# A graph layer's sorted edge groups, taken in ten pairs and in quarters instead of one by one and in halves

## The chip, the cores and the metric

The kernel runs on one core of a Trainium2 chip. The time is the device time of one execution in microseconds, as the median of several runs. The engines are TensorE (PE in the profile, its weight loads PEld), VectorE (DVE), ScalarE (ACT), GpSimd (POOL) and SyncE (SP). Each has a queue of its own and works through it in order.

## The reference

There are 6,250 nodes with 128 features and 100,000 edges, sorted by their destination `dst`. Each edge has a source `src` and four attributes.

```python
msg_in = concatenate([x[src], x[dst], edge_attr], axis=1)
h = silu(msg_in @ mW1 + mb1)
messages = h @ mW2 + mb2
aggregated = segment_sum(messages, dst, num_segments=N)
u = silu(concatenate([x, aggregated], axis=1) @ uW1 + ub1)
updated = u @ uW2 + ub2
out = layernorm(x + layer_norm(x + updated, ln_g, ln_b))
```

## The kernel before

**Tables.** The product with mW1 is split by rows of mW1: the source part of all nodes is a table `A` (and `tab_a` in memory), the destination part with the bias a table `tab_b`. An edge's hidden row is the silu of its row of `A`, its row of `tab_b` and the product of its attributes.

**Groups.** The edges are cut into 98 groups of 1,024 (`G` = 8 tiles of 128). 78 of them are *listed* groups: GpSimd gathers their rows of `tab_a` by eight indirect DMAs a group (`fetch`, line 244), the destination and attribute parts are products of a window of 80 rows of `tab_b` with a matrix of zeros and ones (`before_rows`, tile `pre`), VectorE adds both (`hidden`, line 665) and ScalarE takes the silu (line 667). Every other of GpSimd's gathers is tied to one of TensorE's products (`paced`), so that gathers go on with the products.

**Sorted groups.** The other 20 groups, every fourth from 15 to 91, have no gather. Their edges were sorted by source on the chip, in order over four rows of 256, and their rows of `A` are selected by products. `A` is held in three bf16 parts (`parts_of`). The windows of sorted positions in which the 128 nodes of block `b` can fall are given by `window`; for each the three parts are multiplied by a mask `O` of zeros and ones, and the sums collect in the bank `po`. `picks` makes the masks: two rows of four by VectorE (line 1065), two by ScalarE with a Square and one common Relu (lines 1069 and 1070). `sorted_matrices` (lines 1047 and 1056) compares for the destinations (`st`) and for the edges' places (`Oc`); `attribute_part` brings the attributes into sorted order by a product with `Oc` and masks it into `st` (line 1081); `begin_half` opens `po` with the destination and attribute parts; `select` runs the selection; `sorted_hidden` takes the silu of `po` (line 1112); `turned_hidden` transposes it back to rows of edges (`h_s`, line 1121); `sorted_oh` makes the matrix for the sums by destination.

**Sums.** `sums` multiplies a group's hidden rows by its matrix `oh` into the tile `pt` (80 columns, or 104 for listed groups; beside them the transposed degrees, when they are due), and `add` adds it into the nodes' sums (`acc`, line 713) and counts (line 707).

**Order.** The order is written out by hand (`manual_schedule`): one stage of the loop (line 1225) for each listed group `g`. In a stage the engines' queues get, in this order: loads and gathers for groups some stages ahead; `matrices` of the listed group two ahead; `before_rows` and `hidden` of the next one; the sorted groups' steps (`sorted_before`); the sums of `g`; more of the sorted groups' steps (`sorted_behind`); and the steps of a batch of 512 nodes (`node_stage`: `node_u`, `node_y` and `node_z` in three following stages, and for a later batch `load_x`, `turned_x` and `make_b`). With one sorted group to three listed ones, each sorted group's steps are spread over six stages; `d` is how many stages are left until its sums. At `d` = 3 the first half is selected (48 and 36 products), at 2 the third quarter of the masks (39), at 1 the fourth (45). At `d` = 0 its sums stand ahead of those of `g`.

**Banks.** The product tiles are `pre` (three banks), `pn` (two, function `bank`), `po` and `pt` (one each).

Names of products in the profile: line 152 is the helper `matmul`, line 155 the helper `transpose`.

Of the kernel before, what the change touches and what calls it, by code (L numbers as in the profile page):

```python
# [10 lines left out]
F32 = mybir.dt.float32  # L11
# [16 lines left out]
def kernel(  # L28
# [57 lines left out]
    Q0, QD, QN = 15, 4, 20  # L86
    by_sort = {Q0 + QD * q: q for q in range(QN)}
# [6 lines left out]
    SORTED = Q0 - 7  # L94
    S0 = 96
    HB = GE // 2
    SLACK = 400.0
# [13 lines left out]
    def made_for(g):  # L111
        stage = stage_of(g) - 5 if g in by_sort else turn_of(g) - LEAD
        return max(k for k in range(NB) if k < 2 or x_stage(k) + 2 < stage)
# [5 lines left out]
    def window(b, half):  # L119
# [4 lines left out]
        lo = max(floor(edge(b * P, -1)), half * HB)  # L124
        hi = min(ceil(edge(min(b * P + P - 1, N - 1), 1)) + 1, half * HB + HB)
        return lo, hi
# [48 lines left out]

    def narrow():
        return ps1.tile([P, 2 * P], F32, name="pt")
# [396 lines left out]
    for k in range(NST + 1):  # L574
        ohbuf.append(kept.tile([P, G, WS if k < NST else W], F32, name=f"oh{k}"))
# [258 lines left out]
    def turned_lists():  # L834
        pt = selected()
        for f, of in enumerate((src_i, rel)):
            picked = first.tile([P, QN, G], F32, name="picked")
            nc.vector.tensor_copy(picked, of[:, Q0 : Q0 + QN * QD : QD, :])
# [135 lines left out]
    def prepare():  # L974
        pool = edges.enter_context(tc.tile_pool(name="sel", bufs=1, side="right"))
        t = {
            "O": lambda: pool.tile([P, G // 2, HB], BF16, name="O", bufs=3),
            "sc": lambda: pool.tile([P, 2, GE], F16, name="sc", bufs=2),
            "ar": lambda: pool.tile([P, GE], F16, name="ar"),
            "h": lambda: pool.tile([P, G, H], F32, name="h_s"),  # L980
            "hT": lambda: pool.tile([P, HB], F32, name="hT", bufs=2),
        }
        t["Oc"] = pool.tile([P, GE], F32, name="Oc")
        t["st"] = pool.tile([P, GE], F32, name="st_s")
        t["mv"] = [pool.tile([P, H], F32, name=f"mv_s{k}") for k in range(2)]
        t["at"] = pool.tile([P, P], F32, name="at_s")
        nc.vector.memset(t["st"][S0 - 32 : S0], 0.0)
        for m in t["mv"]:
            nc.vector.memset(m[S0 - 32 : S0], 0.0)
        nc.vector.memset(t["at"][:, :S0], 0.0)  # L990
# [34 lines left out]
    def load_sorted(g):  # L1025
        t, q = sel[0], by_sort[g]
        cols = slice(q * GE, (q + 1) * GE)
        now["sc", g] = t["sc"]()
        nc.sync.dma_start(
            now["sc", g], sd[0:2, cols].rearrange("(o f) e -> o f e", o=1).to_broadcast([P, 2, GE])  # L1030
        )
        now["ar"] = t["ar"]()
        nc.sync.dma_start(now["ar"][:W], sd[3:4, cols].to_broadcast([W, GE]))
        nc.sync.dma_start(now["ar"][S0:], sd[2:3, cols].to_broadcast([P - S0, GE]))
        nc.sync.dma_start(
            t["at"][:, S0:],
            edge_attr[g * GE : (g + 1) * GE].rearrange("(c a) d -> c (a d)", a=G),
        )

    def load_rows(g):  # L1040
        t, q = sel[0], by_sort[g]
        need_bases(g)
        nc.sync.dma_start(t["mv"][q % 2][:W], tab_b[bass.ds(bases[g], W), :])

    def sorted_matrices(g):
        t = sel[0]
        nc.vector.tensor_scalar(
            t["st"][:W],
            now["ar"][:W],
            p_col[:W],  # L1050
            0.0,
            op0=OP.is_equal,
            op1=OP.add,
            accum_out=deg_col(g),
        )
        nc.vector.tensor_scalar(t["Oc"], now["sc", g][:, 1], p_col, None, op0=OP.is_equal)

    def picks(g, c):
        half, r0 = c // 2, c % 2 * (G // 2)
        O = sel[0]["O"]()  # L1060
        key = now["sc", g][:, 0, half * HB : (half + 1) * HB]
        for j in range(G // 2):
            r = r0 + j
            if j < 2:
                nc.vector.tensor_scalar(  # L1065
                    O[:, j], key, p_rows[:, r : r + 1], None, op0=OP.is_equal
                )
            else:
                nc.scalar.activation(O[:, j], key, AF.Square, bias=p_less[:, r : r + 1])  # L1069
        nc.scalar.activation(O[:, 2:], O[:, 2:], AF.Relu, bias=ones[:, 0:1], scale=-1.0)  # L1070
        now[c] = O
# [4 lines left out]
    def attribute_part(half):  # L1076
        t = sel[0]
        cols = slice(half * HB, (half + 1) * HB)
        px = bank().rearrange("p i f -> p (i f)")
        matmul(px, t["at"], t["Oc"][:, cols], start=True, stop=True)  # L1080
        nc.vector.scalar_tensor_tensor(
            t["st"][S0:, cols], now["ar"][S0:, cols], part[S0:], px[S0:],
            op0=OP.is_equal, op1=OP.mult,
        )

    def begin_half(g, half):
        t = sel[0]
        now["po"] = selected()
        matmul(
            now["po"], t["mv"][by_sort[g] % 2], t["st"][:, half * HB : (half + 1) * HB], start=True, stop=False  # L1090
        )

    def select(c):
        half, r0 = c // 2, c % 2 * (G // 2)
        O, po = now.pop(c), now["po"]
        todo = []
        for b in range(NT):
            if r0 <= b % G < r0 + G // 2:
                lo, hi = window(b, half)
                if lo < hi:  # L1100
                    todo.append((b, lo - half * HB, hi - half * HB))
        for i, (b, lo, hi) in enumerate(todo):
            for a in parts_of(b):
                last_one = c % 2 == 1 and i == len(todo) - 1 and a.tensor is sel[0]["low"].tensor
                matmul(
                    po[:, lo:hi], a, O[:, b % G - r0, lo:hi],
                    start=False, stop=last_one, share=1 / 3,
                )

    def sorted_hidden(half):  # L1110
        now["hT", half] = sel[0]["hT"]()
        nc.scalar.activation(now["hT", half], now.pop("po"), AF.Silu)  # L1112

    def turned_hidden(g, half):
        if half == 0:
            h_s[g] = sel[0]["h"]()
        px = bank().rearrange("p i f -> p (i f)")
        hT = now.pop(("hT", half))
        for i in range(G // 2):
            transpose(px[:, i * P : (i + 1) * P], hT[:, i * P : (i + 1) * P], ident)  # L1120
        nc.scalar.copy(
            h_s[g][:, half * G // 2 : (half + 1) * G // 2].rearrange("p i f -> p (i f)"), px
        )

    def sorted_oh(g):
        oh[g] = ohbuf[NST]
        nc.vector.tensor_tensor(
            oh[g][:, :, :W],
            w_row[:, None, :].to_broadcast([P, G, W]),
            rel_s[:, by_sort[g], :, None].to_broadcast([P, G, W]),  # L1130
            op=OP.is_equal,
        )

    def sorted_ahead(j):
        for k in by_sort:
            if j == stage_of(k) - 6:
                load_sorted(k)
            if j == stage_of(k) - 5:
                load_rows(k)

    def sorted_first(j):
        for k in by_sort:
            if stage_of(k) == j:
                turned_hidden(k, 1)

    def sorted_before(j):
        for k in by_sort:
            d = stage_of(k) - j
            if d in (5, 4, 3, 2):
                picks(k, 5 - d)  # L1150
        for k in by_sort:
            if stage_of(k) == j:
                add(k, sums(k))
        for k in by_sort:
            d = stage_of(k) - j
            if d == 4:
                attribute_part(0)
            if d == 3:
                begin_half(k, 0)
                select(0)  # L1160
                select(1)
                sorted_hidden(0)
            if d == 2:
                turned_hidden(k, 0)
                begin_half(k, 1)
                select(2)
            if d == 1:
                select(3)
                sorted_hidden(1)
                sorted_oh(k)  # L1170

    def sorted_behind(j):
        for k in by_sort:
            d = stage_of(k) - j
            if d == 4:
                attribute_part(1)
        for k in by_sort:
            d = stage_of(k) - j
            if d == 5:
                sorted_matrices(k)  # L1180
# [44 lines left out]
    for j, g in enumerate(listed):  # L1225
# [19 lines left out]
        sorted_first(j)  # L1245
# [320 lines left out]
```

## Time and profile before

| | us |
|---|---|
| median of 3 runs (lowest, highest) | 1009.2 (1008.7, 1020.3) |
| profiled execution, its time | 1011.3 |
| its span, first to last instruction | 1009.2 |
| TensorE busy in the span | 802.7 |
| GpSimd busy in the span | 611.0 |
| VectorE busy in the span | 583.9 |
| ScalarE busy in the span | 459.0 |

The mean granted clock of TensorE is 0.893 over the span. Rows of groups of instructions give the line, engine, operation, output<-input, shapes and count, then busy us and the mean ns of one, then the engine's idle time just before them and what ended it. Rows of waits give who waited for whom, us in total, times, and the longest one. Rows of a window give its start and end, its length, each engine's busy us with the number of instructions, TensorE's granted clock, the busy share of the DMA engines and GB/s. Rows of the timeline give start, length, engine, line and what was done how many times in a row; those of the chain give start, length and what stood in the chain. "issue" is time in which an engine waited for nothing that the profile shows.

### The profile page before, as it was taken

The page shows a single profiled execution, that of the slowest core. Times are in us where ns is not written, and L with a number is a line of the kernel's source. Part 1 is how long each engine was busy: PE and PEld are TensorE (multiplying, and loading weights), DVE is VectorE, ACT ScalarE, POOL GpSimd, SP SyncE. Part 2 cuts the span into 40 slices and gives each one's busy share as a digit, 9 for nine tenths or more (in the row PEclk, how much of TensorE's full clock was granted, in tenths as well). Part 3 has the DMA queues.
Part 4 walks back from the last instruction along what each step waited for, and adds up shares of the span by engine and source line. Part 5 has one row for each costly group of instructions (what it writes and reads, how often), then busy time and mean ns, then how long its engine had stood idle before and what let it go on. Part 6 is the DMA issues. An engine that isn't in the chain of part 4 may idle for free.

```text
span 1009.2 us, 19469 instructions
## 1 busy us (share of the span) xinstructions
PE 802.7 (80%) x7141; PEld 694.4 (69%) x7141; DVE 583.9 (58%) x1467; ACT 459.0 (45%) x690; POOL 611.0 (61%) x633
## 2 busy tenths in 40 slices
PE   4557546778988978978889878988888889888784
PEld 4547546667867777767768777777777677677673
DVE  3465687964654654745655664763754664664473
ACT  1122113563545545545554554563554554453343
POOL 6656655866666666665666566666665666675550
PEclk8769777889999989989999999989999989998875
DMA  9543222442333433432332432432432423321220
GB/s 228 156 107 99 77 59 80 112 114 64 112 93 87 115 89 90 113 88 79 110 111 66 126 104 64 127 102 72 130 90 76 124 81 96 96 78 51 67 57 26
DMA packets 87784, 96.27 MB, mean 95 GB/s; under 512 B 22070, under 2 KB 63622, under 8 KB 87682
## 3 DMA queue, kind: packets, MB, share of 16 engines
q1 hardware_dynamic: 54410, 47.59, 16.2%
q0 software_dynamic: 19904, 40.80, 16.1%
q10 hardware_dynamic: 13368, 6.56, 2.4%
q8 instruction: 58, 0.95, 0.4%
q14 instruction: 44, 0.36, 0.1%
HBM read 83.26 MB, written 11.63 MB: 94 GB/s over the span
## 4 chain that ended last, share of the span: by engine, by line
PE 63%; issue 14%; DVE 13%; ACT 4%; another core or an unknown queue 3%; DMA 1%; DVEq 1%; POOL 0%; ACTq 0%; SPq 0%; POOLq 0%
PE po L152 22%; PE pt L152 16%; PE pre L152 12%; PE pn L152 9%; PE pn L155 2%; DVE ga L665 1%; ACT O L1069 1%; ACT O L1070 1%; DVE y L773 1%; DVE bn L726 1%; DVE z L798 1%; DVE deg L707 1%; DVE st L613 1%; ACT h L667 1%
## 5 line engine op out<-in xcount | busy, mean ns | idle before, releaser
L244 POOL DMA_INDIRECT ga<-tab_a,src_i x582 | 570.7, 981 | 348.1 <-issue 163.4
L152 PE MATMUL po<-O,A_low 128*128 128x144 bf16 (+25 forms) x1120 | 208.7, 226 | 20.3 <-issue 20.0
L152 PE MATMUL po<-O,A 128*128 128x147 bf16 (+37 forms) x1720 | 174.3, 227 | 39.0 <-issue 20.3
L152 PE MATMUL pre<-mv,st 128*128 128x128 f32 x1244 | 178.0, 292 | 28.6 <-issue 7.8
L152 PEld LDWEIGHTS pre<-mv,st 128*128 128x128 f32 x1244 | 163.8, 206 | 41.0 <-issue 21.1
L152 PEld LDWEIGHTS pt<-oh,h 128*128 128x128 f32 x1244 | 170.2, 215 | 29.0 <-issue 26.2
L152 PE MATMUL pt<-oh,h 128*128 128x104 f32 x1244 | 177.3, 300 | 13.8 <-issue 10.1
L713 DVE TENSOR_TENSOR acc<-acc,pt 128x80 f32 x98 | 23.0, 235 | 283.4 <-PE pt L152 197.2
L667 ACT ACTIVATE h<-ga 128x512 f32<-128x512 f32 x146 | 89.0, 627 | 213.3 <-DVE ga L665 106.6
L152 PEld LDWEIGHTS <-A 128*128 128x128 bf16 x1720 | 141.5, 104 | 56.0 <-issue 54.7
L152 PEld LDWEIGHTS <-A_low 128*128 128x128 bf16 x1120 | 114.3, 103 | 24.6 <-issue 24.3
L665 DVE TENSOR_TENSOR ga<-ga,pre 128x512 f32<-128x512 f32 x146 | 94.6, 676 | 36.9 <-PE po L152 11.0
L613 DVE TENSOR_SCALAR_CACHE_REDUCE st<-near,p_rows 80x1024 f32<-80x1024 f16 x78 | 98.5, 1262 | 13.0 <-issue 10.9
L1069 ACT ACTIVATE O<-sc,p_less 128x512 bf16<-128x512 f16 x160 | 105.5, 706 | 0.0
L1070 ACT ACTIVATE O<-O,ones 128x1024 bf16<-128x1024 bf16 x80 | 91.8, 1148 | 2.6
L1112 ACT ACTIVATE hT<-po 128x512 f32<-128x512 f32 x40 | 23.5, 587 | 120.2 <-PE po L152 46.1
L152 PE MATMUL po<-O,A_high 128*128 128x51 bf16 (+12 forms) x520 | 52.2, 221 | 15.8 <-issue 15.5
L623 DVE TENSOR_TENSOR oh<-w_row,rel 128x640 f32<-128x640 f32 x78 | 63.6, 815 | 0.6
L152 PEld LDWEIGHTS <-A_high 128*128 128x128 bf16 x520 | 38.5, 100 | 35.1 <-issue 35.1
L244 POOL DMA_INDIRECT ga<-in_x_dram,src_i x40 | 38.5, 963 | 22.3 <-issue 9.3
L152 PE MATMUL pn<-Oc,at_s 128*128 128x512 f32 x80 | 46.5, 661 | 6.9 <-issue 6.6
L1065 DVE TENSOR_SCALAR O<-sc,p_rows 128x512 bf16<-128x512 f16 x160 | 50.5, 367 | 0.0
(229 smaller groups left out, 910.1 us busy)
## 6 DMA issues: line engine op xcount, KB each, us to landing
near<-near_d SPq DMA_DIRECT2D x78, 160.0 KB
sc<-sd SPq DMA_DIRECT2D x20, 512.0 KB
ga<-tab_a,src_i POOLq DMA_INDIRECT x582
ar<-sd SPq DMA_DIRECT2D x20, 160.0 KB
mv<-tab_b SPq DMA_DIRECT2D x78, 40.0 KB
tab_a<-A SPq DMA_DIRECT2D x11, 256.0 KB
tab_b<-o SPq DMA_DIRECT2D x11, 256.0 KB
out_dram<-o ACTq DMA_DIRECT2D x11, 256.0 KB
```

The lines of the kernel that those rows point to most:

```text
L152: counted(nc.tensor.matmul(to, *operands, **flags), to, share)
L155: counted(nc.tensor.transpose(to, *operands), to)
L244: ins = nc.gpsimd.indirect_dma_start(out=rows[g][:, i, :], out_offset=None, in_=x if g < RAW else tab_a[:, :], in_offset=bass.IndirectOffs ...
L613: nc.vector.tensor_scalar(stbuf[turn_of(g) % NST][:W], near.pop(g), p_col[:W], 0.0, op0=OP.is_equal, op1=OP.add, accum_out=deg_col(g),)
L623: nc.vector.tensor_tensor(oh[g][:, :n, :W], w_row[:, None, :].to_broadcast([P, n, W]), rel[:, g, :n, None].to_broadcast([P, n, W]), op=OP. ...
L665: nc.vector.tensor_add(s[:, i], s[:, i], of)
L667: nc.scalar.activation(h[:, i], of, AF.Silu)
L713: nc.vector.tensor_add(to, to, pt[:, :W])
L1065: nc.vector.tensor_scalar(O[:, j], key, p_rows[:, r : r + 1], None, op0=OP.is_equal)
L1069: nc.scalar.activation(O[:, j], key, AF.Square, bias=p_less[:, r : r + 1])
L1070: nc.scalar.activation(O[:, 2:], O[:, 2:], AF.Relu, bias=ones[:, 0:1], scale=-1.0)
L1112: nc.scalar.activation(now["hT", half], now.pop("po"), AF.Silu)
```

## The change

The sorted groups are now ten pairs of neighbours: 17 and 18, 25 and 26, up to 89 and 90, with six listed groups between pairs. A pair is worked on together and by quarters of 256 sorted positions: a bank of `po` holds one quarter of both groups, and a product of `select` takes the columns of both at once, so that one load of weights serves two pieces of columns. The quarters are selected at `d` = 5, 4, 2 and 1. Three stages ahead of its selection a quarter's values are loaded, two stages ahead it is compared, one stage ahead its attribute product and its masks are made, and one stage behind it is turned back. Within a stage, turning back and the attribute product come ahead of the comparisons and the selection. The sums of both groups come behind the sums of `g`. The tile `pt` becomes two halves of one bank that take turns. The comparisons by quarters write their counts into `deg_p`, which is added up at the end. Masks get four buffers instead of three; `st`, `at` and the matrices `oh` of sorted groups get two, `ar` two, and `Oc` is half as wide.

```diff
-    Q0, QD, QN = 15, 4, 20
-    by_sort = {Q0 + QD * q: q for q in range(QN)}
+    Q0, QD, QN = 17, 8, 20
+    firsts = [Q0 + QD * q for q in range(QN // 2)]
+    by_sort = {k + u: 2 * q + u for q, k in enumerate(firsts) for u in range(2)}
...
+    QB = GE // GR
+    at_stage = (5, 4, 2, 1)
...
+    narrow_ps = ps1.tile([P, 2, 2 * P], F32, name="pt")
+    sides = [0]
+
     def narrow():
-        return ps1.tile([P, 2 * P], F32, name="pt")
+        sides[0] = 1 - sides[0]
+        return narrow_ps[:, sides[0]]
...
-    def load_sorted(g):
...
+    def load_part(k, u):
+        t = sel[0]
+        q = by_sort[k]
+        of = sd[:, q * GE : (q + 2) * GE].rearrange("f (g r c) -> f g r c", g=2, r=GR)[:, :, u, :]
+        sc = now["sc", u] = t["sc"]()
+        ar = now["ar", u] = t["ar"]()
+        for f in range(2):
+            nc.sync.dma_start(
+                sc[:, f], of[f].rearrange("(o g) c -> o g c", o=1).to_broadcast([P, 2, QB])
+            )
...
+    def load_rows(k):
+        for v in range(2):
+            need_bases(k + v)
+            nc.sync.dma_start(sel[0]["mv"][v][:W], tab_b[bass.ds(bases[k + v], W), :])
...
+    def sorted_matrices(k, u):
         t = sel[0]
+        for v in range(2):
+            nc.vector.tensor_scalar(
+                t["st"][u % 2][:W, v * QB : (v + 1) * QB], now["ar", u][:W, v], p_col[:W], 0.0,
+                op0=OP.is_equal, op1=OP.add, accum_out=t["deg"][:, v, u : u + 1],
+            )
+        now["Oc"] = t["Oc"]()
         nc.vector.tensor_scalar(
+            now["Oc"], now["sc", u][:, 1].rearrange("p g c -> p (g c)"), p_col, None, op0=OP.is_equal
+        )
+        if u == GR - 1:
+            for v in range(2):
+                nc.vector.tensor_reduce(deg_col(k + v), t["deg"][:, v], AX.X, OP.add)
...
-    def attribute_part(half):
+    def attribute_part(u):
         t = sel[0]
-        cols = slice(half * HB, (half + 1) * HB)
         px = bank().rearrange("p i f -> p (i f)")
-        matmul(px, t["at"], t["Oc"][:, cols], start=True, stop=True)
+        picks(u)
+        for v in range(2):
+            cols = slice(v * QB, (v + 1) * QB)
+            matmul(px[:, cols], t["at"][v], now["Oc"][:, cols], start=True, stop=True)
...
+    def select(u):
         t = sel[0]
+        po = now["po"] = selected()
+        for v in range(2):
+            cols = slice(v * QB, (v + 1) * QB)
+            matmul(po[:, cols], t["mv"][v], t["st"][u % 2][:, cols], start=v == 0, stop=False)
+        to = po.rearrange("p (g c) -> p g c", g=2)
         todo = []
...
+        for part_r in range(2):
+            O = now.pop(("O", u, part_r)).rearrange("p r (g c) -> p r g c", g=2)
+            r0 = part_r * (G // 2)
+            for b in range(NT):
+                if r0 <= b % G < r0 + G // 2:
+                    lo, hi = window(b, u)
+                    if lo < hi:
+                        cols = slice(lo - u * QB, hi - u * QB)
+                        for a in parts_of(b):
+                            todo.append((to[:, :, cols], a, O[:, b % G - r0, :, cols]))
+        for n, (to, a, of) in enumerate(todo):
+            matmul(to, a, of, start=False, stop=n == len(todo) - 1, share=1 / 3)
...
+    def pair_at(j, d):
+        return [k for k in firsts if stage_of(k) - j == d]
+
     def sorted_ahead(j):
+        for u, d in enumerate(at_stage):
+            for k in pair_at(j, d + 3):
+                load_part(k, u)
+        for k in pair_at(j, 7):
+            load_attributes(k)
+        for k in pair_at(j, 6):
+            load_rows(k)
 
     def sorted_before(j):
+        for u, d in enumerate(at_stage):
+            for k in pair_at(j, d - 1):
+                turned_hidden(k, u)
+        for u, d in enumerate(at_stage):
+            for _ in pair_at(j, d + 1):
+                attribute_part(u)
+        for u, d in enumerate(at_stage):
+            for k in pair_at(j, d + 2):
+                sorted_matrices(k, u)
+        for u, d in enumerate(at_stage):
+            for _ in pair_at(j, d):
+                select(u)
+                sorted_hidden(u)
+        for k in pair_at(j, 1):
+            for v in range(2):
+                sorted_oh(k + v)
 
     def sorted_behind(j):
+        for k in pair_at(j, 0):
+            for v in range(2):
+                add(k + v, sums(k + v))
```

More of the change, by code (lines that the diff above doesn't have):

```diff
@@ L117, in ahead, with window @@
         return listed[i] if i < len(listed) else NG
-    def window(b, half):
+    def window(b, quarter):
         def edge(node, sign):
@@ L1058, in picks @@
[L1058 to L1071, printed above, removed]
+            ar[S0:], of[2].rearrange("(o g) c -> o g c", o=1).to_broadcast([P - S0, 2, QB])
+        )
@@ L1093, in select @@
-    def select(c):
-        half, r0 = c // 2, c % 2 * (G // 2)
-        O, po = now.pop(c), now["po"]
-        todo = []
[L1097 to L1108, printed above, removed]
```

165 lines of the change are left out of this document (67 added, 98 removed).

## The prediction

> **What bounds the kernel now.** I read the page's busy times, its slices and its chain first; then the middle as one window; then TensorE's waits there; then the timeline of the selection; and last VectorE's instructions around the node steps. A "pair" below is two sorted groups with the six gathered ones around them: six stages of the loop in both kernels.
>
> ```profile
> PE 802.7 (80%) x7141; PEld 694.4 (69%) x7141; DVE 583.9 (58%) x1467; ACT 459.0 (45%) x690; POOL 611.0 (61%) x633
> ...
> PE 63%; issue 14%; DVE 13%; ACT 4%; another core or an unknown queue 3%; DMA 1%; DVEq 1%; POOL 0%; ACTq 0%; SPq 0%; POOLq 0%
> 230.00:950.00 720.00, 619.88 (x5987) 531.78 (x5986) 407.06 (x974) 367.30 (x549) 450.02 (x464) 0.94 0.34 94
> 242.02 1.06 PE L152 MATMUL po<-st_s,mv_s 128*128 128x512 f32 x2
> 874.04 1.06 PE L152 MATMUL po<-st_s,mv_s 128*128 128x512 f32 x2
> ```
>
> TensorE leads the chain and is busy 620 of the middle's 720 us, at a mean granted clock of 0.94 (the third number from the right of the window's row). The last two rows open the selections of groups 19 and 87, which are 17 sorted groups apart: 632.0/17 = 37.2 us each, 74.4 us a pair, so the middle is 9.7 pairs. What TensorE waits for there:
>
> ```profile
> PE po L152 <- issue: 52.2, 99, 1.2
> PE po L152 <- ACT O L1070: 17.8, 9, 2.3
> PE pre L152 <- issue: 6.3, 6, 3.9
> PE pn L155 <- DVE st_s L1081: 5.3, 4, 2.4
> PE pt L152 <- issue: 3.9, 7, 0.8
> PE pn L155 <- issue: 3.8, 6, 1.4
> PE pn L152 <- issue: 2.9, 3, 1.2
> ```
>
> Half of the 100 us of waiting is "issue" ahead of selection products: pauses of about half a microsecond for which no releaser is seen. They stand in the long run of the first half, where two selections of 48 and 36 products follow each other:
>
> ```profile
> 428.00 3.13 PE po L152 x47
> 431.14 0.15 issue
> 431.29 0.20 PE po L152 x2
> ...
> 427.90:437.70 9.80, 7.73 (x89) 0.84 0.35 97
> 506.90:511.70 4.80, 4.80 (x86) 1.00 0.48 147
> 442.50:444.80 2.30, 2.30 (x41) 1.00 0.12 29
> ```
>
> The same 84 products (the counts take in a few neighbours) took 9.8 us with pauses and 4.8 without; the run of 39 products in the second half shows none. The pauses come when many short products, each with its weight load, follow each other for more than some 2.3 us. DMA doesn't decide it: its share was 0.48 in the run without pauses and 0.35 in the one with them.
>
> **The change, part by part.**
>
> *Selection: fewer products, the same columns.* Adding up window() gives 56 windows and 6,529 columns for one group cut in halves, and 70 windows with 6,529 columns for each of two groups cut in quarters. Three parts each: 336 products a pair become 210, each with twice the columns. What a column costs:
>
> ```profile
> 508.36 0.30 PE L152 MATMUL po<-O,A 128*128 128x154 bf16 x2
> ...
> 508.56 0.30 PE L152 MATMUL po<-O,A 128*128 128x155 bf16 x2
> 509.37 0.20 PE L152 MATMUL po<-O,A 128*128 128x36 bf16 x2
> 509.44 0.19 PE L152 MATMUL po<-O,A 128*128 128x14 bf16 x2
> ```
>
> Three products of 154 columns start within 0.20 us (0.067 each, 0.435 ns a column); three of 36 within 0.07 (0.023 each). The wide ones go by columns and gain nothing; only narrow ones stand on a floor. Summed over all windows by these two figures the pair stays at 17.3 us, less 0.06 for the narrow ones: **-0.1 a pair**. That operands now come in two pieces I cost at nothing; bounds are 0 and that floor again on 210 products (4.8 us), and I take 0, since it is nearest to the wide products, whose time is in their columns alone.
>
> *The pauses.* A quarter has 48, 57, 57 and 48 products, in 3.7 to 5.0 us by 0.435 ns a column: 11 to 13 starts a microsecond, where the run that pauses has 84 in 4.5, 18 to 19 a microsecond, and the 39-product run the same rate for a shorter time without a pause. So both the rate and the length in excess fall. Ends: none left, or all 52.2/9.7 = 5.4 us a pair. I take 0.8, nearer to the quiet short run: **-4.6**. Of the other four issue rows, 16.9 us in all and of the same look, I take half: 16.9/9.7/2 = **-0.9**; ends 0 and -1.7.
>
> *Masks made earlier.* picks() for a whole quarter now stands in the stage ahead of its select, four times in six stages, and in none that holds node_z. ScalarE's work is the same count: 16 squares and 8 Relus a pair.
>
> ```profile
> L1069 ACT ACTIVATE O<-sc,p_less 128x512 bf16<-128x512 f16 x150 | 98.9, 706 | 0.0
> L1070 ACT ACTIVATE O<-O,ones 128x1024 bf16<-128x1024 bf16 x75 | 86.1, 1148 | 2.4
> 403.32 1.79 PE pre L152 x16
> 426.26 1.75 PE pt L152 x16
> 459.40 0.94 PE pn L152 x2
> ```
>
> A quarter's masks take 4 x 0.71 + 2 x 1.15 = 5.1 us, against a TensorE stage of 5 (the one stage with neither selection nor pair sums) to 11 us. The second mask of the quarter behind that short stage is ready about 2 us before its products come up. So the O wait goes: 17.8/9.7 = **-1.8**. If that cover is missing, it stays. The transposes that waited for st_s (5.3 us) stand ahead of the attribute product now: **-0.5**.
>
> *VectorE: more small work, and one new wait.* Comparisons come by quarter:
>
> ```profile
> L1047 DVE TENSOR_SCALAR_CACHE_REDUCE st_s<-ar,p_rows 80x1024 f32<-80x1024 f16 x18 | 22.8, 1269 | 0.0
> L1056 DVE TENSOR_SCALAR Oc<-sc,p_rows 128x1024 f32<-128x1024 f16 x18 | 14.6, 813 | 0.0
> L713 DVE TENSOR_TENSOR acc<-acc,pt 128x80 f32 x77 | 18.0, 234 | 242.4 <-PE pt L152 170.8 <-PE pre L152 26.0 <-PE pn L152 19.8
> 441.56 1.12 DVE L773 SCALAR_TENSOR_TENSOR y<-y,var,g_b 128x128 f32<-128x128 f32 x4
> 445.46 0.18 DVE L727 BATCH_NORM_AGGREGATE var<-bn 128x2 f32<-128x6 f32 x1
> 449.30 1.27 DVE L613 TENSOR_SCALAR_CACHE_REDUCE st<-near,p_rows 80x1024 f32<-80x1024 f16 x1 [3.66 <-issue]
> 451.35 1.29 DVE ga L665 x2
> ```
>
> With about 0.15 us fixed (most of an 80-element add's 0.23), 1,024 elements in 1.27 become four of 0.43, and Oc's 0.81 becomes two of 0.48: about +2 us a pair with the reductions of deg. VectorE waits 242 us in the middle ahead of acc, 25 us a pair, which covers this everywhere but in one place. The node steps keep their stages, so node_z falls on the stage of quarter 1's selection, and behind it comes the short stage; the comparisons of the last quarter stand at that stage's end, and TensorE needs them early in the next, since the attribute product is ahead of the selection. From the adds at the end of the node_z stage, VectorE has: node_z 4.1 us (441.56 to 445.64), st and oh 2.05 (449.30 to 451.35), two ga adds 1.2, picks 1.05, the attribute mask 0.7, comparisons 1.3: 10.4. TensorE has to its attribute product: two `pre` of 1.8, `pt` 1.75, an attribute product 0.9, eight transposes 0.9: 7.2. It waits 3.2, and 0.8 on average for the register load that sometimes stands between (the 3.66 above). Ends: 0 (where TensorE is late itself) and 6.9 (the load each time). **+4.0 a pair.** Queued behind that product are the whole selection and the stage's sums.
>
> *Moved behind, and double sums.* The pair's sums stand behind the listed group's, in the other half of a bank; they wait for nothing new (h is copied at the stage's start). Ends 0 and 2 x 0.23 less; I take 0.
>
> *Transfers.* A pair has 16 part loads, two of attributes and two of rows on SyncE, 20 for 10 before. Each row of 2 KB becomes four of 512 B: 368 packets a sorted group become 1,472.
>
> ```profile
> q1 hardware_dynamic: 54410, 47.59, 16.2%
> SPq L446 <- DVE st L613: 119.8, 8, 17.8
> L244 POOL DMA_INDIRECT ga<-tab_a,src_i x582 | 570.7, 981 | 348.1 <-issue 163.4
> 437.05 0.95 POOL L244 DMA_INDIRECT ga<-tab_a,src_i  x1 [0.30 <-issue]
> ```
>
> At that queue's 48 ns a packet, 22,080 more are 6.6% of the 16 engines, on 34%: covered. A part load waits for the masks two quarters back, a stage earlier, and near, mv and st of a gathered group queue behind it; they are due a stage later, and SyncE has waited up to 17.8 us in front of them already without TensorE waiting for near. Cost 0; if that cover goes, one landing, some 3 us. Gathers are not reduced: 48 a pair at 0.95 and 0.30 us idle ahead, 1.25 from start to start, are 60 us, a floor that isn't reached.
>
> *Clock.* A mean of 0.94 loses 0.06 x 74.4 x 0.86 busy = 3.8 us a pair. The run without pauses had 1.00, that with them 0.84. I take 0.96 behind the change: 2.5, **-1.3**. Ends 0 and -3.8.
>
> *Sum:* -0.1 - 4.6 - 0.9 - 1.8 - 0.5 + 4.0 - 1.3 = -5.2, so 69.2 us a pair; ten pairs: -52. What lies before and behind the pairs stays. The profiled execution took 1011.3 us (span 1009.2), 2 above the median of the runs: 1011.3 - 52 = 959; against the median that is 50 less, or 5%.
>
> **The rivals.**
>
> *All waits go.* VectorE's new wait is hidden, pauses and cold clock vanish: -0.1 - 5.4 - 1.7 - 1.8 - 0.5 - 3.8 = -13.3, or 61.1 a pair, just above the gathers' floor: 1011 - 133 = 878. For it: VectorE's 25 us of slack. Against: it is slack at another place than needed.
>
> *The change doesn't do what it says: pauses stay.* They may hang on something else than the density of products. Then pauses, their clock and the rows behind them stay: -0.1 - 1.8 - 0.5 + 4.0 = +1.6, or -2.4 without the new wait: 1027 or 987, 1007 in the middle. For it: the run at 506.90 has the same density and no pause. Against: the short runs' silence. The Trainium skill, "TensorE: Matmul & The Clock Gate", section "Wait — 56ns, not 53.3ns?", speaks for this rival: matmuls start N/2.4 ns plus some 2.5 apart, and never under about 25 ns, so halving the instructions at equal columns should give next to nothing. The rows at 508.36 and 509.37 agree with it; that the same 84 products take 4.8 or 9.8 us is not in it. By it alone, the sum would be the 987 to 1027 above.
>
> *Slower: every quarter waits for VectorE.* If each of the four attribute products waited as I expect of one, the waits were 16 a pair, not 4: 69.2 + 12 = 81.2, and 1011 + 68 = 1079. It decides from 4.0 + 5.2 = 9.2 us of such waits a pair; from 11.2 it is over 2% slower. For it: VectorE's work rises while the pair shortens. Against: the other three have longer stages and no node_z ahead.
>
> **How the numbers follow.** Forecast 959, chance 0.58, own range 919 to 988 (the wait from 0 to 6.9, the rest as taken). All waits go: 0.17. Pauses stay: 0.18. Slower: 0.07. The range 910 to 1005 leaves out the outer half of the first rival and of the second, and the third. 2%, 20 us, is about what a measurement of this kernel can tell from no change, as one of its three runs was 11 us off. Faster: 0.58 + 0.17 = 0.75; within 2%: 0.17; slower: 0.07 and the worst of the second rival, 0.08.
>
> **What would show it.** Pauses: TensorE's waits for issue ahead of po under 15 us. Masks: no wait for O. New wait: TensorE's pn product waits for Oc, some 4 us, once a pair. Clock: above 0.94. Columns: products of 300 columns starting 0.13 us apart; if they start later, two pieces cost something. If waits for sc, ar or near appear, the transfers weren't covered; with a wait for Oc four times a pair the slower rival has come.

## The result and the profile after

The changed kernel is slower: 1095.7 us as the median of four runs (1090.8 to 1098.7) against 1013.4 for the kernel before in the same set of runs, a ratio of 1.080 [1.071, 1.089]. The forecast was 959 us. The profiled execution took 1098.7 us, its span 1096.9. Ratios leave out runs that took over 1.5% longer than the fastest of the same kernel; three experiments have some, and the profile of the kernel before with its sums behind is of such a run, of 1071.4 us.

In the changed kernel the helper `matmul` is line 155 and `transpose` line 158; `add` is line 720, `hidden` 672, the comparisons of `sorted_matrices` 1072 and 1082, `picks` 1096, 1100 and 1101, the mask of the attribute product 1114, the silu of `po` 1142, the copy to `h_s` 1153. The window of the middle and two rows of its timeline that open the first quarters of two pairs, four pairs apart:

```profile
230.00:950.00 720.00, 587.61 (x4366) 509.64 (x4365) 382.75 (x1016) 334.82 (x499) 398.53 (x414) 0.84 0.33 86
```

```profile
459.21 1.03 PE L155 MATMUL po<-st_s,mv_s 128*128 128x256 f32 x4
...
794.15 1.03 PE L155 MATMUL po<-st_s,mv_s 128*128 128x256 f32 x4
```

A pair takes 334.9/4 = 83.7 us, against 74.4 before and 69.2 forecast; the middle is 8.6 pairs. TensorE's clock fell from 0.94 to 0.84, although fewer products are issued. What TensorE waits for there:

```profile
PE pn L158 <- DVE st_s L1114: 32.4, 7, 6.8
PE pt L155 <- DVE acc L720: 26.9, 13, 7.7
PE pt L155 <- issue: 20.5, 37, 1.2
PE pt L155 <- DVE st_s L1072: 20.4, 4, 5.8
PE po L155 <- issue: 18.5, 32, 1.1
PE pre L155 <- issue: 5.8, 10, 0.8
PE pn L158 <- DVE O L1096: 2.8, 1, 2.8
PE pn L155 <- issue: 2.6, 3, 1.0
...
```

The pauses ahead of `po` fell and the wait for ScalarE's mask is gone. But the sums in `pt` wait 26.9 + 20.4 us, which the kernel before did not do in this window, and they now have pauses of their own. The timeline of the last stage of one pair shows why. First TensorE, then VectorE (start, length, engine, line, what, how often, and in brackets the idle time ahead with its releaser); the first row of each list is of the pair before:

```profile
441.69 3.70 PE L155 MATMUL pt<-oh,h_s 128*128 128x80 f32 x16 [5.82 <-DVE st_s L1072]
...
521.97 0.69 PE L155 MATMUL pt<-oh,h 128*128 128x104 f32 x4 [0.36 <-issue]
526.78 3.70 PE L155 MATMUL pt<-oh,h_s 128*128 128x80 f32 x16 [4.12 <-DVE acc L720]
530.81 3.70 PE L155 MATMUL pt<-oh,h_s 128*128 128x80 f32 x16 [0.33 <-DVE acc L720]
```

```profile
441.40 0.24 DVE L720 TENSOR_TENSOR acc<-acc,pt 128x80 f32 x1
...
522.02 1.28 DVE L672 TENSOR_TENSOR ga<-ga,pre 128x512 f32<-128x512 f32 x2 [2.57 <-remote]
523.22 1.13 DVE L1096 TENSOR_SCALAR O<-sc,p_rows 128x512 bf16<-128x512 f16 x4
524.38 0.76 DVE L1114 SCALAR_TENSOR_TENSOR st_s<-ar,part,pn 32x512 f32<-32x512 f16 x1
525.17 0.47 DVE L1072 TENSOR_SCALAR_CACHE_REDUCE st_s<-ar,p_rows 80x256 f32<-80x256 f16 x1
...
525.98 0.48 DVE L1082 TENSOR_SCALAR Oc<-sc,p_rows 128x512 f32<-128x512 f16 x1
526.49 0.24 DVE L720 TENSOR_TENSOR acc<-acc,pt 128x80 f32 x1
```

TensorE ends the sums of the listed group at 522.66. The pair's sums come next in its queue and write the other half of the same bank, but they start only when VectorE has read the first half, at 526.49 to 526.73; and VectorE reaches that add behind two ga adds, the masks, the attribute mask and the comparisons of the next pair. From 522.02 it works through them in 4.7 us with hardly a gap. It also began late: it had stood idle for 2.57 us ahead of the ga adds ("remote" is a queue that the trace doesn't name), and for 1.2 to 3.1 us in this stage of four other pairs. So a part of the wait is that late start, whose cause was not followed up. The row at 441.69 names a comparison, but it is the same wait: the product starts 0.05 us behind the end of the add at 441.40. So the two rows for `pt` in the list, 47.3 us, are one cause. (The Trainium skill, "PSUM — Partial Sum Buffer", section "PSUM bank collisions raise a hardware error", says that two engines have to be kept apart by bank and quadrant of partitions (32 of the 128), and that another address of the same bank still collides. The 4.12 us of this row agree: the other half was no help.) The halves are one tile of the program, and no run here parts the bank from the tile as what the wait goes by. The two sums then take 3.70 us each instead of 1.91 in the kernel before, of which this is one:

```profile
426.09 1.91 PE L152 MATMUL pt<-oh,h_s 128*128 128x80 f32 x16
```

The clock, by windows of this stretch of the changed kernel:

```profile
511.00:523.00 12.00, 9.03 (x71) 7.93 (x69) 6.39 (x15) 3.31 (x8) 6.88 (x8) 1.00 0.49 118
523.10:543.60 20.50, 16.49 (x55) 12.23 (x56) 6.63 (x18) 7.41 (x11) 7.05 (x8) 0.50 0.20 55
543.60:571.00 27.40, 24.12 (x220) 21.67 (x219) 17.62 (x54) 12.70 (x20) 17.35 (x18) 1.00 0.34 93
```

The half clock lasted 20.5 us, with TensorE busy for 16.5 of them. It began at 523.1, only 0.44 us into the wait; in the 3.4 us ahead of that TensorE was busy for 1.6, because the sums of the listed group had pauses. So at this place the fall stands behind pauses and wait together.

### The profile page after: what moved, and what is told of

Read it like the earlier page. It is cut to its first block, busy times and chain, and to the rows that moved or that the text cites. A ratio compares the mean times of both kernels' runs of the same rounds, so it can differ in the third digit from the quotient of the medians.

```text
span 1096.9 us, 17579 instructions
## 1 busy us (share of the span) xinstructions
PE 846.5 (77%) x6041; PEld 733.4 (67%) x6041; DVE 600.0 (55%) x1629; ACT 458.8 (42%) x690; POOL 607.9 (55%) x633
## 4 chain that ended last, share of the span: by engine, by line
PE 60%; DVE 16%; issue 10%; POOL 2%; another core or an unknown queue 2%; ACT 1%; DMA 1%; DVEq 1%; SPq 0%; ACTq 0%; POOLq 0%
PE po L155 19%; PE pt L155 16%; PE pre L155 13%; PE pn L155 9%; DVE ga L672 2%; PE pn L158 2%; POOL ga L251 2%; DVE O L1096 2%; DVE oh L630 1%; DVE st L620 1%; DVE st_s L1114 1%; DVE y L780 1%; DMA ga<-tab_a,src_i 1%; DVE z L805 1%
## 5 line engine op out<-in xcount | busy, mean ns | idle before, releaser
L155 PE MATMUL pre<-mv,st 128*128 128x128 f32 x1244 | 196.4, 314 | 28.5 <-issue 15.4
L155 PEld LDWEIGHTS pre<-mv,st 128*128 128x128 f32 x1244 | 184.7, 228 | 45.4 <-issue 33.9
L155 PEld LDWEIGHTS pt<-oh,h 128*128 128x128 f32 x1244 | 161.3, 203 | 34.6 <-issue 32.5
L155 PE MATMUL po<-O,A_low 128*128 128x314 bf16 (+54 forms) x700 | 156.3, 246 | 8.1 <-issue 7.9
L155 PE MATMUL po<-O,A 128*128 128x216 bf16 (+37 forms) x1060 | 146.2, 248 | 12.4 <-issue 12.2
L155 PEld LDWEIGHTS <-A 128*128 128x128 bf16 x1060 | 89.6, 98 | 36.0 <-issue 21.1
L155 PE MATMUL pt<-oh,h_s 128*128 128x80 f32 x320 | 72.4, 419 | 50.7 <-DVE acc L720 27.5
L155 PEld LDWEIGHTS pt<-oh,h_s 128*128 128x128 f32 x320 | 68.1, 323 | 55.4 <-DVE acc L720 30.5
L155 PEld LDWEIGHTS <-A_low 128*128 128x128 bf16 x700 | 67.8, 98 | 13.5 <-issue 7.0
L750 ACT ACTIVATE uT<-pn,ub_col 128x512 f32<-128x512 f32 (+1 forms) x12 | 8.1, 679 | 110.7 <-PE pn L155 110.7
L1096 DVE TENSOR_SCALAR O<-sc,p_rows 128x512 bf16<-128x512 f16 x160 | 49.7, 371 | 0.0
```

Source lines behind the costliest of these rows:

```text
L155: counted(nc.tensor.matmul(to, *operands, **flags), to, share)
L1096: nc.vector.tensor_scalar(O[:, j], key, p_rows[:, r : r + 1], None, op0=OP.is_equal)
```

## The experiments

Theory A: the pair's sums, placed behind those of the listed group in one bank, wait for an add that stands late in VectorE's queue, and the clock falls over that wait. A second wait, smaller, is the forecast one behind `node_z`. The rivals are told in each expectation. Ratios are to the kernel before in the same set of runs; they are not compared between chips on which that kernel takes another time: 842 us on the chips of the first eight runs below, 1010 to 1012 on those of the others.

**Two banks, and its controls.** To have a bank free, `w_row` goes to other memory; the second kernel below does this alone; the third has `pt` as one tile as before, without `bufs=2`.

```diff
-    w_row = ps1.tile([P, W], F32, name="w_row")
+    w_row = consts.tile([P, W], F32, name="w_row")
...
-        sides[0] = 1 - sides[0]
-        return narrow_ps[:, sides[0]]
+        return ps1.tile([P, 2 * P], F32, name="pt", bufs=2)
```

> The tile of the sums, pt, gets two banks that take turns (the bank is had by keeping w_row out of product memory). Theory A, the pair's sums wait for the listed group's add because both halves of pt lie in one bank, and TensorE's clock falls over that wait: the first of the pair's sums no longer waits, the second waits some 2 us for the listed group's add; a pair goes from 84 to about 78 us, 1030 to 1050 us in all. Theory B, the time is lost behind the node steps (pn waits for st_s, 32 us): within 10 us of the changed kernel, 1085 to 1105.

> Only w_row is kept out of product memory, pt stays as in the changed kernel: the control for the run with two banks. Both theories: within 10 us of the changed kernel, 1085 to 1105; if the comparisons for oh (0.82 us each) become faster or slower, by their 98 times that difference at most.

> pt is one tile again, as before the change, all else as in the changed kernel. Theory A, two halves of one bank give no turn: within 10 us of the changed kernel, 1085 to 1105. If the halves do let sums and adds overlap, it is slower than the changed kernel by up to ten times 4 us, 1135.

Measured: two banks 918.3 us, 1.093 [1.087, 1.099]; `w_row` alone 965.5, 1.145 [1.137, 1.153]; one tile 969.2, 1.151 [1.144, 1.157]. The two halves of one bank give nothing, two banks some 5%, 47 us less than `w_row` alone, where theory A had 46 to 66. The wait for the add falls from 39.3 us, in both controls, to 13.6 in the same window of 670 us.

**The next pair's work behind the sums.** In the pair's last stage the attribute product of the next pair's quarter 0 and the comparisons of its quarter 1 are issued behind the three sums:

```diff
     def sorted_behind(j):
         for k in pair_at(j, 0):
             for v in range(2):
                 add(k + v, sums(k + v))
+        for _ in pair_at(j, 6):
+            attribute_part(0)
+        for k in pair_at(j, 6):
+            sorted_matrices(k, 1)
```

> In the stage of the pair's sums alone, the attribute product with its masks and the comparisons go behind the three sums, so that VectorE comes to each add at once. Theory A: the waits of pt for acc and st_s (47.6 us) fall to some 10, the clock stays up in that stage, and the time falls to 970 to 1000 us. Theory B: the node steps' wait is untouched, 1080 to 1100 us.

Measured: 904.4 us, 1.074 [1.067, 1.082]; that is some 60 us less than the controls of the same set, half of the loss on this chip, but short of the 96 to 126 us that theory A asked for. The wait for the add falls to 17.9 us, not to 10.

**Second wait.** Both kernels again on another chip, then `node_z` one stage later (`if j == u + 3`), and that together with the edit above.

> The kernel before, profiled beside the three that follow. In the last four runs the kernel before took 842 us where it had taken 1009, and TensorE's waits in those four show no pauses for issue. Both theories: 1.00 of itself; if the pauses belong to the chip and not to the kernel, its profile has none either, and a pair of sorted groups takes some 58 to 60 us where it took 74.

> The changed kernel, on the same chip as the others of this call. Where there are pauses, 1.08 of the kernel before; where there are none, 1.14 to 1.16, as the two runs that differ from it only in where w_row and pt lie.

> Of the changed kernel only node_z goes one stage later, behind the short stage instead of ahead of it. Theory B (VectorE is late behind the node steps): the wait of pn for st_s, 4.1 to 4.7 us a pair, and the half clock behind it, some 3, go: 70 to 80 us less than the changed kernel. Theory A alone (only the pair's sums cost): within 15 us of it.

> Both: the pair's sums ahead of the attribute product in their stage, and node_z one stage later. If the two waits and the clock that falls over them are the whole loss, it is level with the kernel before where that has no pauses (0.98 to 1.03, as the gathers' 48 times 1.25 us a pair are a floor for both), and 0.88 to 0.95 of it where it has them. If something else in the change costs time (two pieces of columns, small transfers), it stays above 1.05.

Measured: before 841.5, after 968.0, 1.150 [1.145, 1.156]; `node_z` later 966.2, 1.148 [1.142, 1.154]; both edits 891.7, 1.059 [1.054, 1.065]. TensorE's waits from 200 to 800 us in the kernel before, after, and with `node_z` later:

```profile
PE po L152 <- ACT O L1070: 20.0, 9, 2.3
PE pre L152 <- DVE st L613: 5.9, 2, 3.1
PE pn L155 <- ACT hT L1112: 3.6, 6, 0.7
...
```

```profile
PE pn L158 <- DVE st_s L1114: 36.9, 8, 4.7
PE pt L155 <- DVE acc L720: 35.4, 16, 6.4
```

```profile
PE pt L155 <- DVE acc L720: 35.5, 16, 6.4
PE pn L158 <- ACT hT L1142: 34.8, 7, 5.4
...
```

Three things follow. Moving `node_z` only hands the second wait from VectorE to ScalarE, whose silu of `po` stands behind the 5 us of masks; the 70 to 80 us of theory B did not come. With both edits the time stayed above 1.05, as it should if something else costs; the next experiments look for it at ScalarE. And on this chip the kernel before has no row of "issue" ahead of products at all, nor has the changed one: the pauses that were to be the gain belong to the chip or its host, not to the program alone. The clock falls here too, without pauses: in this window its mean is 0.98 in the kernel before and 0.87 in the changed one, so waits are enough for it.

**Work into the wait.** Twenty products that nothing reads are put between the sums of the listed group and those of the pair. Work is added, nothing is taken away:

```diff
         for k in pair_at(j, 0):
+            fill = selected()
+            for i in range(20):
+                nc.tensor.matmul(fill[:, :P], u2, w2, start=True, stop=True)
             for v in range(2):
                 add(k + v, sums(k + v))
```

> The changed kernel with 20 products of 128 columns, whose result nobody reads, between the sums of the listed group and those of the pair, some 4.4 us at full clock. TensorE works through its wait instead of idling. If half of what the pair's sums cost is the clock that falls over the wait: the clock stays up, the pair's sums take 1.8 us instead of 3.7, and the time falls by 40 to 70 us although work was added. If the wait alone is the cost: no change, or up to 20 us slower.

Measured: 1065.6 us, 1.057 [1.050, 1.064]: faster than the changed kernel, whose ratios on chips with pauses were 1.080 and, on this chip, 1.091. That is some 34 us, less than the 40 to 70 expected. Its timeline at the same place (each filling product counts as two), and its window of the middle:

```profile
511.76 6.28 PE L1201 MATMUL po<-w,u 128*128 128x128 f32 x40
517.88 1.91 PE L155 MATMUL pt<-oh,h_s 128*128 128x80 f32 x16
520.12 2.01 PE L155 MATMUL pt<-oh,h_s 128*128 128x80 f32 x16 [0.33 <-DVE acc L720]
```

```profile
230.00:950.00 720.00, 625.11 (x4966) 552.78 (x4965) 399.35 (x1068) 347.97 (x519) 418.60 (x436) 0.91 0.35 90
```

The filling takes 2 us more than the wait did, and the sums behind it run at full clock, 1.91 instead of 3.70 us: the clock is a good part of the price. Here too the clock falls behind the pauses, but it is back after 3.4 us: 0.50 from 511.9 to 515.2, within the filling, and 1.00 from 515.3. So the pauses were enough to start this fall; with the wait behind them it lasted 20.5 us.

**Masks behind the silu.** So that ScalarE isn't late, the masks of the next quarter are made behind `sorted_hidden` in the stages of quarters 0 and 2. This is tried on top of both edits, with two banks too, and without moving `node_z`:

```diff
-        picks(u)
+        if u not in (1, 3):
+            picks(u)
...
                 sorted_hidden(u)
+                if u in (0, 2):
+                    picks(u + 1)
```

> Sums first and node steps one stage later, as in the run with both; besides, in the two stages that hold a selection and the next quarter's masks, the masks go behind the silu of the quarter just selected. In the run with both, TensorE waited 4.8 us a pair for that silu, which stood behind 5 us of masks on ScalarE. If that order was the wait: the wait goes, with the half clock behind it, and a pair goes from 67.7 to 61 or 62 us: 0.97 to 1.00 of the kernel before where that has no pauses. If ScalarE's work as such is too much, the wait moves to the masks (po waits for O) and it stays at 1.04 to 1.06.

> The same with two banks for pt that take turns (w_row kept out of product memory). The waits of pt for acc are down to some 1.3 us a pair in the run with both; this takes most of them: 5 to 15 us less than without the two banks.

> Sums first and masks behind the silu, but node_z in its old stage. Theory: the wait of the second half bank pn for st_s behind node_z, 4.6 us a pair, is still there, since VectorE causes it and not ScalarE; 1.06 to 1.08 of the kernel before. If the masks alone were it, as fast as with node_z later.

Measured: 1.026 [1.020, 1.032]; with two banks 1.003 [0.999, 1.006]; with `node_z` in its old stage 1.059 [1.053, 1.066]. So the second wait is worth some 3% once ScalarE is free to take `node_z`'s place. What the place of the masks is worth by itself is not shown: the run with both edits alone was on a chip without pauses, these on one with them.

**The order of the sums by itself.** All experiments so far left the pair's sums behind. Now the changed kernel with only these put ahead of the attribute product again, the same in the best version so far, and the reverse: in the kernel *before*, the sums of a sorted group go behind those of `g`. (In that last one the sorted groups' degrees are added from the block that was transposed for a later group; the number of adds stays, but its counts are not those of the reference.)

```diff
     def sorted_before(j):
         for u, d in enumerate(at_stage):
             for k in pair_at(j, d - 1):
                 turned_hidden(k, u)
+        for k in pair_at(j, 0):
+            for v in range(2):
+                add(k + v, sums(k + v))
...
     def sorted_behind(j):
-        for k in pair_at(j, 0):
-            for v in range(2):
-                add(k + v, sums(k + v))
```

> The changed kernel as it is, for its ratio to the kernel before on the chip of these runs: 1.08 where the kernel before takes some 1010 us and TensorE pauses for issue, 1.15 where it takes some 842 us.

> The changed kernel with one thing undone: the pair's sums stand ahead of the attribute product, the comparisons and the sums of g, as the sums of a sorted group did before. Theory A (the sums behind wait for an add that stands late in VectorE's queue, and the clock falls over that wait): VectorE has only two ga adds and the node steps ahead of these adds, so the pt <- acc wait falls from some 35 to under 15 us, and the ratio to the kernel before falls by 0.06 to 0.09 below that of the changed kernel. Rival (three sums in a row in one bank wait wherever they stand): the wait stays over 25 us and the ratio falls by under 0.03.

> The sums ahead, node_z a stage later, the masks of the next quarter behind the silu, and two banks for pt. Theory A: the waits pt <- acc and pn <- st_s are both gone; on a chip without pauses 0.99 to 1.04 of the kernel before (the gathers' floor of 60 us a pair is close), with pauses 0.96 to 1.01, as the selection's own pauses are fewer. Rival (the order of the sums doesn't matter once pt has two banks): the same ratio as with the sums behind, 1.00 where there are pauses.

> The kernel before with one part of the change alone: the sums of a sorted group stand behind those of g instead of ahead of the selection. Theory A: the sums follow the add of g at once; in that stage VectorE has the ga adds and the node steps but no comparisons and no picks in its queue, so 0.5 to 3 us a sorted group at 20 groups, ratio 1.01 to 1.07. Rival (the order of sums costs nothing, as the prediction had it): 0.995 to 1.005.

Measured: after 1.091 [1.086, 1.096]; sums ahead 1.067 [1.059, 1.074]; the best version with sums ahead 1.020 [1.016, 1.024], where it had 1.003 with sums behind; before with sums behind 1.044 [1.035, 1.053]. The reverse shows the loss in the old kernel: its waits ahead of `pt` come to 55.1 us in the middle, where the kernel before has 3.9. Its TensorE and VectorE rows at one such place:

```profile
535.66 1.97 PE L152 MATMUL pt<-oh,h 128*128 128x104 f32 x16
541.10 3.67 PE L152 MATMUL pt<-oh,h_s 128*128 128x80 f32 x16 [3.48 <-issue]
```

```profile
539.67 0.24 DVE L713 TENSOR_TENSOR acc<-acc,pt 128x80 f32 x1 [8.52 <-remote]
539.93 1.03 DVE L707 TENSOR_TENSOR deg<-deg,pt 1x80 f32 x4
```

Sums that follow each other in one bank cost a wait even where VectorE is idle: here they wait for the add and four counts, and run at half clock behind it. Why that add started 2 us behind the end of the sums was not followed up. The list of waits calls the 3.48 us "issue"; that it ends 0.14 us behind the last count suggests that it waited for the counts.

The direct undo did less than expected, 0.024 instead of 0.06 to 0.09. Its waits and ScalarE's timeline:

```profile
PE pn L158 <- DVE st_s L1114: 49.0, 8, 7.1
PE pt L155 <- ACT h_s L1153: 40.1, 9, 6.0
...
PE pt L155 <- DVE acc L720: 3.6, 9, 0.4
...
```

```profile
512.69 0.63 ACT L674 ACTIVATE h<-ga 128x512 f32<-128x512 f32 x1 [0.68 <-DMA ga<-tab_a,src_i]
513.23 0.57 ACT L1153 COPY h_s<-pn 128x512 f32<-128x512 f32 x1
```

The wait for the add fell to 3.6 us, as theory A had it, while the wait behind `node_z` grew from 32.4 to 49.0. The sums now wait for ScalarE's copy of the last quarter, which the change had also moved: it stands behind the silu of a listed group, and that one waits for a gather to land. In the kernel before, `sorted_first` had these transposes at the very start of the stage. Put there again:

```diff
         sorted_ahead(j)
+        for k in pair_at(j, 0):
+            turned_hidden(k, 3)
```

> The pair's sums ahead, as in the run before, where the acc wait went to 3.6 us but the sums then waited 40.1 us for ScalarE's copy of the last quarter (h_s, 9 times); now its transposes stand at the very start of the stage, ahead of the listed group's products, as they did before the change. Theory A (that copy was only too late by its place): the h_s wait falls under 8 us, 3 to 4 us a pair go with some cold clock, ratio to the kernel before 1.02 to 1.05 on a chip with pauses, against 1.0665. Rival (ScalarE is behind with its queue whatever the place): the wait stays over 25 us or the transposes wait for hT instead, ratio over 1.055.

> The same place for the transposes in the kernel with node_z a stage later, the masks behind the silu and two banks, which stood at 1.0201 with an h_s wait of 37.1 us in the middle (7 times). Theory A: that wait falls under 8 us, some 4 us of 73 a pair, ratio 0.97 to 0.995, the first version ahead of the kernel before where there are pauses. Rival (ScalarE is the next bound): the wait is named hT or h instead and the ratio stays at 1.005 to 1.025.

Measured: 1047.4 us, 1.036 [1.030, 1.043], against 1.091 of the changed kernel; with all the other edits 1005.8 us against 1011.6, 0.992 [0.988, 0.996]. In the former the wait for the copy is down from 40.1 to 0.8 us. The latter's longest waits in the middle:

```profile
PE po L155 <- issue: 33.4, 63, 1.2
PE pt L155 <- issue: 19.0, 32, 2.2
PE pt L155 <- DVE acc L716: 12.3, 5, 5.9
PE pn L158 <- ACT h L670: 8.5, 4, 3.1
PE pn L155 <- DVE Oc L1078: 8.2, 4, 3.3
...
```

So on a chip with pauses the pairs are level with the kernel before, at best 1% ahead, once the longest waits that came with the new order are taken away; of the 102 us of waiting that are left, 63 are pauses. This version also has two banks for `pt` and `node_z` a stage later, which the kernel before lacks, so what the pairs alone are worth is not shown. On a chip without pauses it was not run.

## Why the prediction was wrong

By its own steps, per pair, from the window rows and waits of the middle (9.7 pairs before, 8.6 after):

| step | forecast | measured |
|---|---|---|
| issue, all rows | -4.6 - 0.9 = -5.5 | 69.1/9.7 to 47.4/8.6: -1.6 |
| masks, wait for ScalarE's O | -1.8 | 17.8/9.7 to 0: -1.8 |
| st_s transposes and the new wait | -0.5 + 4.0 = +3.5 | 5.3/9.7 to (32.4 + 2.8)/8.6: +3.5 |
| pair's sums moved behind, halves of a bank | 0 | 0 to 47.3/8.6: +5.5 |
| columns and clock, by TensorE's busy time | -0.1 - 1.3 = -1.4 | 619.9/9.7 to 587.6/8.6: +4.4 |
| smaller rows | | -0.5 |
| sum | -5.2 | +9.5 (83.7 - 74.4 = 9.3) |

*The step that failed* is "Moved behind, and double sums": "they wait for nothing new (h is copied at the stage's start). Ends 0 and 2 x 0.23 less; I take 0." The sums wait for the add of the sums ahead of them in the same bank, 5.5 us a pair; the step's two ends, 0 and 0.46 us less, allowed a gain and no cost. The kernel before kept the selection between its two sums, which was the cover, and a step costed at nothing should have named it. The sentence in brackets was wrong too: the copy was no longer at the stage's start, as the run with the sums ahead showed. The failure is worth more than its 5.5 us, because of the half clock around the wait: the busy time, forecast to shrink, grew by 4.4 us. How much of that goes with this wait and how much with the next one is not parted, but with this wait filled some 34 us went over ten pairs, though no work was saved. With sums and transposes back in their old places the ratio falls from 1.091 to 1.036, and with the wait filled by idle work to 1.057.

*The new wait of VectorE* was of the forecast size, once a pair. Its place was slightly off: it stands in the short stage itself, and not the attribute product waits for Oc, but the transposes of `x` behind it wait for the `pn` bank which the late attribute mask still has to read. Two rows of the chain:

```profile
573.36 0.77 DVE st_s L1114
...
574.18 1.12 PE pn L158 x4
```

The row `pn <- DVE O L1096` (2.8 us, once) is the same wait of another pair, put down to the masks just ahead of the attribute mask. The forecast priced the wait alone; the half clock behind it was left out here too.

*The pauses*: ahead of `po` they fell from 5.4 to 2.2 us a pair, two thirds of the forecast gain; 18.5 us are left, where under 15 was the sign. The forecast read their cause from three runs of products. Over the whole middle of the kernel before, 2 of the 19 long runs of 84 have no pause, 4 of the 20 runs of 39 have one, 1.6 to 1.9 us behind their start, and 11 of the 20 runs of 45 have some. So "more than some 2.3 us" is no bound; and on the chip without pauses the same program has none. That they may hang on something else was the second rival's condition, and it is met in part. But the sums, which hardly had any, got 20.5/8.6 = 2.4, so the other issue rows grew instead of halving. What makes the pauses is open; the section on the hardware has what was seen of them.

*Masks* and *transfers* went as forecast: no wait for ScalarE's masks and none for sc, ar or near is in the list. *Columns*: the forecast's figure holds; the selection ahead of the stage shown above starts three products of 204 columns within 0.27 us:

```profile
512.75 0.34 PE L155 MATMUL po<-O,A 128*128 128x204 bf16 x2
512.93 0.25 PE L155 MATMUL po<-O,A_low 128*128 128x204 bf16 x1
513.02 0.32 PE L155 MATMUL po<-O,A 128*128 128x186 bf16 x2
```

That is 0.090 us each, and 204 x 0.435 ns are 0.089: two pieces cost nothing.

The rival on the slower side, every quarter waiting for VectorE (1079 us), came near the time by chance: its mechanism did not come, the wait stood once a pair.

## What to carry to other kernels

Where an edit brings two users of one accumulator bank next to each other, find what stood between them: that was the cover, and two halves of a bank didn't replace it here. Follow the reader's queue up to its read and the producer's queue up to its copy, since a moved step takes its place behind whatever that engine is doing. And price a wait of about 4 us on TensorE with the half clock around it: here the busy time grew by 4.4 us a pair, for 9.0 us more of such waits.

## What the runs showed of the hardware

The half clock lasted far longer than the wait: 20.5 us around 4.12 us of idle time, 16.5 of them busy. It began 0.44 us into the wait, behind 3.4 us in which TensorE was busy for 1.63. With the wait filled, it began behind the same pauses and lasted 3.4 us. (The Trainium skill, "TensorE: Matmul & The Clock Gate", section "What's actually happening", gives one idle window of some 3.4 us to fall and one busy window to rise. Neither agrees here: the clock fell 0.44 us into the idle time, behind a stretch that was busy for half, and TensorE was at work from 526.78 on, 16.5 us of the 16.8 to 543.6, while the window shows 0.50 for all of it.)

The kernel before took 842 us in two sets of runs, on two chips, and 1010 to 1013 in all others. Where a profile of it was taken, it had 52.2 us of issue rows ahead of `po` where it took 1011 us and none where it took 840. The changed kernel stood at 1.15 of it where there were no pauses and at 1.08 to 1.09 where there were, which fits with a gain that can only be had from the pauses, but does not show it.
